# More attention beside each layer block, with the depthwise convolution of that stage on VectorE

## The chip, the cores and the metric

The kernel runs on one core of one Trainium2 chip. A core has five engines with a queue each, which they work off in order: TensorE (PE: matmuls, and the loads of its stationary operand, PEld), VectorE (DVE), ScalarE (ACT), GpSimd (POOL) and SyncE (SP, which here only starts transfers). They meet through semaphores. The metric is the device time in microseconds of one launch, the median of several runs; the profile is of one execution.

## The reference, cut to what matters

Two layers follow each other on `x` of shape 4 x 64 x 64 x 256, in float32.

```python
# layer 0 (DIM 256, INNER 384, 8 states, windows of 2 x 2)
xz = layernorm(x) @ in_proj_W
x_proj, z = xz[..., :384], xz[..., 384:]
windows = window_partition(x_proj, 2)                  # 4 tokens each
y_fwd = light_s6(windows, fwd ...)                     # a scan of 4 steps over 8 states
y_bwd = flip(light_s6(flip(windows), bwd ...))
y_ssm = window_unpartition(0.5 * (y_fwd + y_bwd))
y_dw = depthwise_conv_3x3(x_proj, dw_kernel)           # 384 channels, padding SAME
y_conv = gelu(y_dw @ pw_W)
alpha = sigmoid(gate)
y = (alpha * y_ssm + (1 - alpha) * y_conv) * silu(z) @ out_W
x_out = x + y
x1 = x_out + gelu(layernorm(x_out) @ fuse_W1 + fuse_b1) @ fuse_W2 + fuse_b2

# layer 1: self-attention over the 4096 positions of each image
f, g, hh = x1 @ Wf + bf, x1 @ Wg + bg, x1 @ Wh + bh    # 32, 32, 256 columns
attn = softmax(g @ f.T)                                # 4096 x 4096 for each image
out = gamma * ((attn @ hh) @ Wo + bo) + x1
```

A scan step of `light_s6` is state = dA * state + dBx, y = sum over states of state * c, with dA = exp(dt * a).

## The kernel before

**Tiling.** An image is cut into 8 layer blocks of 8 rows, 512 tokens each (32 blocks for the 4 images). The attention of an image is cut by queries: an early query block is 128 queries against all 4096 keys (32 to an image), a late unit is 256 queries (16 to an image).

**The first layer is one generator.** `first_layer` yields after each small piece of work, and each yield carries a cost in microseconds that the author wrote by hand. For a block `at` it runs `scan(at)`, and beside it, by a credit of SHARE times the scan's costs, `side(at)`: that is the depthwise convolution, the gate and the `tail` of the block before (`conv`, `gate`, `tail(at - 1)`), woven with the head of the block after. `tail` is the pointwise product (L626), the gated combination (L639, L642), the output projection (L649, added at L653), the feed-forward (L669, L680, added at L684), then the keys and queries (L693) and the values (L704, stored after L708). After the scan come `inputs` of the next block (L419, L422) and `merge` (L562, L564).

**The scan.** For each of 8 states and both directions, ScalarE makes the exponentials (L406), TensorE transposes them into a PSUM bank (L462), and VectorE reads the bank into p (L470, L474), carries the state (L492) and adds to y (L485). A bank is free for the next transposes when p was read.

**The depthwise convolution.** For each of three groups of 128 channels it has 9 taps. A tap is either a TensorE matmul of 512 columns with a diagonal matrix (L574), summed in a bank of the ring `q0` to `q3` (`aside`), or a VectorE multiply-and-add over a shifted view of the padded rows (L589 for the first, L595). Before the change image 0 does groups 0 and 1 on TensorE and group 2 on VectorE; images 1 to 3 do six taps of group 0 on TensorE, join them to the other three on VectorE (L591), and do groups 1 and 2 on VectorE.

**Attention beside the layer.** A query block has a preparing generator, `weights`, and a weighted sum, `attend`. `weights` makes the score products in two groups of 16 small matmuls (L844), which take all four banks of the ring at once; ScalarE copies them out (L852), VectorE takes the running maximum (L858, L860, L863, L869), and after two transposes (L867, L871) and a copy (L873) VectorE adds the negative maximum (L877) and ScalarE takes the exponential (L878). `attend` has 8 steps. A step loads two value tiles, does four matmuls into the accumulator (L1036), then moves on its own weights generator and that of the next query block by one piece each, and then lets the first layer run for RATE microseconds of its own costs:

```python
def fill(us):
    debt[0] += us
    while debt[0] > 0:
        cost = next(layer, None)
        ...
        debt[0] -= cost
```

So RATE sets how many query blocks lie beside a layer block. An image's attention begins when the layer has gone through that image; when the whole layer is done, what is left of the queries is done in late units (`late_weights`: L935, L943, L948, L973, L974; `attend_late`: L1014), each of 16 value tiles. `outcome` divides by the sum of the weights and adds the rest (L983, L984).

**What sets the order.** The program writes instructions in the order of these generators; a scheduler that works with priorities then fixes each engine's queue before the launch, and places the semaphore waits. The score products carry a high priority (L839). Value tiles (`vt`) come through SP's queue four ahead, out of five buffers.

Of the kernel before, what the change touches and what calls it, by code (L numbers as in the profile page):

```python
# [34 lines left out]
KI = INNER // P  # L35
# [5 lines left out]
CK = DIM // 8  # L41
EPS = 1e-5
SHARE = 1.2
RATE = 7.2


_VECS = [
# [12 lines left out]
def block_then_attention_kernel(  # L60
# [36 lines left out]
    def v(name, i=0, n=1):  # L97
        a = _AT[name][0] + i
        return vec[:, a : a + n]
# [76 lines left out]
    def aside(shape=(P, TOK)):  # L176

        i = turn[0]
        turn[0] = (i + 1) % 4
        return pss.tile(list(shape), F32, tag=f"q{i}", name=f"q{i}")  # L180
# [383 lines left out]
            nc.vector.scalar_tensor_tensor(xc[:, f, :], py, half_a[:, f : f + 1], xc[:, f, :], ALU.mult, ALU.add)  # L564
            yield 1.1

    def depthwise(ydw, dense, taps):

        for f in range(KI):
            if f < dense:  # L570
                pc = aside()
                for tap in range(taps):
                    dy, dx = divmod(tap, 3)
                    nc.tensor.matmul(  # L574
                        pc, lhsT=diags[9 * f + tap], rhs=xp[:, f, dy : dy + ROWS, dx : dx + W],
                        start=(tap == 0), stop=(tap == taps - 1),
                    )
                    if tap % 3 == 2:
                        yield 2.6
                if taps == 9:  # L580
                    nc.scalar.copy(ydw[:, f, :], pc)
                    continue
            o = ydw[:, f, :].rearrange("p (r c) -> p r c", r=ROWS)
            for tap in range(taps if f < dense else 0, 9):
                dy, dx = divmod(tap, 3)
                x_tap = xp[:, f, dy : dy + ROWS, dx : dx + W]
                w_tap = v("dw", 9 * f + tap)
                if tap == 0:
                    nc.vector.tensor_scalar(o, x_tap, w_tap, None, ALU.mult)  # L589
                elif f < dense and tap == taps:  # L590
                    nc.vector.scalar_tensor_tensor(  # L591
                        o, x_tap, w_tap, pc.rearrange("p (r c) -> p r c", r=ROWS), ALU.mult, ALU.add
                    )
                else:
                    nc.vector.scalar_tensor_tensor(o, x_tap, w_tap, o, ALU.mult, ALU.add)  # L595
                if tap % 3 == 2:
                    yield 2.0
# [3 lines left out]
    def conv(at):  # L601
        b = at // NBLK
        ydw = one.tile([P, KI, TOK], F32, tag="ff", name="ydw")
        ydws[at] = ydw
        yield from depthwise(ydw, KI - 1 if b == 0 else 1, 9 if b == 0 else 6)

    def next_head(at):

# [105 lines left out]
    def side(at):  # L714

        if at == 0:
            yield from late_products()
            yield from next_head(0)
            load_head(2)
            return  # L720
        if at >= NBLK:
            yield from weave(conv(at - 1), 24.0, gate(at - 1, False), 5.2)
        else:
            yield from conv(at - 1)
        yield from weave(tail(at - 1), 46.0, next_head(at), 14.0)
        ready["tail"] = at - 1
# [19 lines left out]
    def first_layer():  # L746
# [22 lines left out]
        for at in range(LAST):  # L769
# [20 lines left out]
            yield from merge(at)  # L790
        yield from drain("tail", LAST - 2)
        yield from conv(LAST - 1)
        yield from gate(LAST - 1, False)
        yield from tail(LAST - 1)
# [27 lines left out]
    def load_values(b, q, n):  # L822

        vt = vp.tile([P, 2, DIM + 1], F32, tag="vt", name="vt")
        a = 2 * (n % 2) * (DIM + 1)
        nc.sync.dma_start(
            out=vt.rearrange("p t c -> p (t c)"), in_=vod[b * NBLK + n // 2][:, a : a + 2 * (DIM + 1)]
        )
        vts[b, q, n] = vt
# [53 lines left out]
# [5 lines that stand above are left out]
            if cost is None:  # L888
                debt[0] = 0.0
                break  # L890
            debt[0] -= cost
# [86 lines left out]
    def outcome(b, q, res, sums):  # L978

        i, t = divmod(q, 4)  # L980
        for c, acc in enumerate(sums):
            rg = st.tile([P, 1], F32, tag="rg", name="rg")
            nc.vector.reciprocal(rg, acc[:, DIM : DIM + 1])  # L983
            nc.vector.scalar_tensor_tensor(res[:, c, :], acc[:, :DIM], rg, res[:, c, :], ALU.mult, ALU.add)  # L984
        a = (t % 2) * DIM
        for wr in range(ROWS // 2):
            nc.sync.dma_start(
                out=ov[b, i, t // 2, wr][:, a : a + len(sums) * DIM],
                in_=res[wr * 32 : (wr + 1) * 32].rearrange("p t c -> p (t c)"),
            )  # L990

    def load_rest(b, q, pool, tag, n):
        i, t = divmod(q, 4)
        res = pool.tile([P, n, DIM], F32, tag=tag, name="res")
        nc.sync.dma_start(
            out=res.rearrange("p t c -> p (t c)"), in_=x1d[b * NBLK + i][:, t * DIM : (t + n) * DIM]
        )
        return res
# [23 lines left out]
    def attend(b, q, es, own, beside, following):  # L1022

        res = load_rest(b, q, two, "res", 1)
        acc = pso.tile([P, TOK], F32, tag="pso", name="acc")
        for k in range(NI):
            for h in range(2):
                n = 2 * k + h
                if n + 4 < 2 * NI:
                    load_values(b, q, n + 4)  # L1030
                else:
                    following(n + 4 - 2 * NI)
                vt = vts.pop((b, q, n))
                for s in range(2):
                    a = (2 * h + s) * P
                    nc.tensor.matmul(  # L1036
                        acc[:, : DIM + 1], lhsT=es[k // 2][:, k % 2, a : a + P], rhs=vt[:, s, :],
                        start=(n == 0 and s == 0), stop=(n == 2 * NI - 1 and s == 1),
                    )
            next(own, None)  # L1040
            next(beside, None)
            fill(RATE)
        outcome(b, q, res, [acc])

# [5 lines left out]
    def twice(pieces):  # L1050

        while True:
            for _ in range(2):
                if next(pieces, 0) == 0:
                    return
            yield
# [7 lines left out]
    own = weights(0, 0, es)  # L1064
    for _ in own:
        fill(RATE)
    a = 0
    while True:
        b, q = divmod(a, NQ)
        b1, q1 = divmod(a + 1, NQ)  # L1070
        if q1 == 0:
            until((b1 + 1) * NBLK - 1)
        ahead = []
        late = ready["tail"] == LAST - 1 and q1 % 2 == 0
        if late:
            n0 = (b1, q1 // 2)
            load_late_queries(*n0)
            beside = twice(late_weights(*n0, 0, ahead))
            attend(b, q, es, own, beside, lambda n: load_late_values(*n0, n))
            es = ahead  # L1080
            break
        if q1 == 0:
            quarter(b1, one, "fQ")
        load_queries(b1, q1)
        beside = weights(b1, q1, ahead)
        attend(b, q, es, own, beside, lambda n: load_values(b1, q1, n))
        es, own = ahead, beside
        a += 1
    odd, block = 0, n0
    while block:  # L1090
        after = ensuing(*block)
        beside, ahead = None, []
        if after:
            load_late_queries(*after)
            beside = late_weights(*after, 1 - odd, ahead)
# [93 lines left out]
```

## Time and profile before

| | |
|---|---|
| median of 3 runs | 5259.01 us (5250.38 to 5259.54) |
| the profiled execution | 5265.47 us |
| its span, first to last instruction | 5263.6 us |
| mean granted TensorE clock | 0.978 |
| PE busy / DVE busy / ACT busy | 4955.8 / 4517.3 / 3571.5 us |
| early query blocks, late units | 74 (296 of L878, 4 each), 27 (216 of L974, 8 each) |
| layer block of image 0, alone | 95 us |
| layer block in the mixed stage, 1128 to 4078 us | 147.5 us, mean of 20 |
| L1036, weighted sum, early | 4736 records, 392 ns mean, 1215.4 us busy |
| L1014, weighted sum, late | 3456 records, 919.7 us busy |
| L574, depthwise taps on TensorE | 576 records, 273.4 us busy |
| L595, depthwise taps on VectorE | 496, 743 ns mean, 357.8 us busy |

How to read it: "busy" is the time in which an engine works on at least one instruction. A float32 matmul of this kernel leaves two records. The mean of one matmul is its own length; since matmuls overlap, a stream of them is closer together than that. An idle engine costs nothing by itself; what matters in a stretch is which engine the others wait for. A group's line gives its busy time, its mean, and, after the last bar, how long the engine idled before it and for whom.

### The profile page before, as it was taken

The numbers are of one execution on the slowest core, as the hardware profiler recorded it, in microseconds if no ns is written. First come the engines' busy times: TensorE is split into PE (matmuls) and PEld (weight loads), VectorE is DVE, ScalarE is ACT, GpSimd is POOL, SyncE is SP. The second block draws the span as 40 slices with busy tenths as digits, with TensorE's granted clock in tenths as the row PEclk, the third lists the DMA queues.
The fourth block names the chain that finished last, engine by engine and source line by source line (L and its number), as shares of the span: only waits on it lengthen the run. The fifth ranks groups of instructions, "written<-read, shape, count | busy, mean of one in ns | idle before, by whom it ended". The sixth has DMA issues, their size and how long they took to land. (4 is left out here: it accounts for less than half of the span.)

```text
span 5263.6 us, 76327 instructions
## 1 busy us (share of the span) xinstructions
PE 4955.8 (94%) x27138; PEld 3543.4 (67%) x27138; DVE 4517.3 (86%) x8256; ACT 3571.5 (68%) x5489; POOL 204.0 (4%) x304
## 2 busy tenths in 40 slices
PE   7999998999999999999999999999999999999999
PEld 4565565666666666666666666666666667888887
DVE  7999999999899988998989988898989866666665
ACT  6778778667777767677777767777777635555554
POOL 0000000000000000000000000000000000000000
PEclk8999999999999999999999999999999999999999
DMA  1010011333333333334333333333333344444444
GB/s 48 26 44 19 23 34 34 102 122 115 118 104 119 113 109 115 114 116 118 118 111 106 119 108 111 118 114 118 112 116 104 112 129 146 147 147 147 147 147 139
DMA packets 330284, 554.14 MB, mean 105 GB/s; under 512 B 51504, under 2 KB 85936, under 8 KB 329904
## 3 DMA queue, kind: packets, MB, share of 16 engines
q1 hardware_dynamic: 326384, 545.40, 34.2%
q8 instruction: 214, 3.51, 0.3%
q10 hardware_dynamic: 3520, 3.87, 0.2%
q14 instruction: 166, 1.36, 0.1%
HBM read 490.28 MB, written 58.79 MB: 104 GB/s over the span
## 5 line engine op out<-in xcount | busy, mean ns | idle before, releaser
L1036 PE MATMUL acc<-vt,eq 128*128 128x257 f32 x4736 | 1215.4, 392 | 17.2 <-issue 7.6
L406 ACT ACTIVATE e<-dt,a_sc 128x384 f32<-128x384 f32 x1536 | 853.3, 611 | 272.8 <-PE bank L462 262.5
L1036 PEld LDWEIGHTS acc<-vt,eq 128*128 128x128 f32 x4736 | 875.0, 195 | 234.2 <-issue 107.6
L462 PEld LDWEIGHTS bank<-ident,e 128*128 128x128 f32 x4320 | 521.2, 143 | 319.5 <-issue 113.4
L462 PE MATMUL bank<-ident,e 128*128 128x128 f32 x4320 | 658.9, 279 | 79.1 <-DVE p L474 37.1
L1014 PE MATMUL bank<-vt,eT 128*128 128x257 f32 x2560 | 645.8, 382 | 0.0
L492 DVE SCALAR_TENSOR_TENSOR h<-u,bc,p 128x384 f32<-128x384 f32 x1024 | 613.4, 613 | 0.4
L485 DVE SCALAR_TENSOR_TENSOR y<-h,bc,y 128x384 f32<-128x384 f32 x960 | 589.0, 614 | 3.2 <-ACT y L483 0.4
L474 DVE TENSOR_TENSOR p<-bank,h 128x384 f32<-128x384 f32 x960 | 517.1, 548 | 55.1 <-PE bank L462 54.5
L1014 PEld LDWEIGHTS bank<-vt,eT 128*128 128x128 f32 x2560 | 478.6, 189 | 83.7 <-issue 13.9
L852 ACT COPY eq<-q 128x512 f32<-128x512 f32 x592 | 308.6, 587 | 192.6 <-PE q L844 117.5
L948 DVE TENSOR_TENSOR mx<-mx,eT 128x512 f32<-128x512 f32 x378 | 261.7, 692 | 152.2 <-ACT eT L943 121.3
L878 ACT ACTIVATE eq<-eq 128x1024 f32<-128x1024 f32 x296 | 308.1, 1053 | 103.0 <-DVE eq L877 100.1
L877 DVE TENSOR_TENSOR eq<-eq,nb 128x1024 f32<-128x1024 f32 x296 | 357.4, 1220 | 7.6 <-ACT nb L873 7.4
L595 DVE SCALAR_TENSOR_TENSOR ydw<-xp,vec,ydw 128x512 f32<-128x512 f32 x496 | 357.8, 743 | 1.4
L943 ACT COPY eT<-q 128x512 f32<-128x512 f32 x432 | 221.5, 597 | 194.7 <-PE q L935 194.7
L860 DVE TENSOR_TENSOR mx<-mx,eq 128x512 f32<-128x512 f32 x444 | 306.5, 690 | 38.4 <-ACT eq L852 31.5
L406 ACT ACT_TABLE_LOAD x241 | 309.2, 1283 | 14.4 <-PE bank L462 10.2
L485 DVE SCALAR_TENSOR_TENSOR y<-p,bc,y 128x384 f32<-128x384 f32 x512 | 313.1, 612 | 0.4
L470 DVE SCALAR_TENSOR_TENSOR p<-bank,bc,u 128x384 f32<-128x384 f32 x480 | 291.6, 608 | 21.1 <-PE bank L462 20.6
L973 DVE TENSOR_TENSOR eT<-eT,m 128x1024 f32<-128x1024 f32 x216 | 247.7, 1219 | 42.3 <-ACT m L970 42.3
L626 PE MATMUL q<-ydw,wpw 128*128 128x512 f32 x576 | 269.5, 602 | 13.3 <-ACT eq L852 12.8
(154 smaller groups left out, 7524.7 us busy)
## 6 DMA issues: line engine op xcount, KB each, us to landing
vt<-vod SPq DMA_DIRECT2D x1616, 257.0 KB, 2.8
vod<-vst SPq DMA_DIRECT2D x32, 514.0 KB, 3.9
xt<-in_x_dram SPq DMA_DIRECT2D x256, 64.0 KB, 1.9
xo<-in_x_dram SPq DMA_DIRECT2D x256, 64.0 KB, 2.3
x1d<-xo SPq DMA_DIRECT2D x32, 512.0 KB, 2.9
res<-x1d SPq DMA_DIRECT2D x74, 128.0 KB, 2.6
out_dram<-res SPq DMA_DIRECT2D x296, 32.0 KB, 1.6
fgd<-fg SPq DMA_DIRECT2D x32, 256.0 KB, 2.1
```

The source lines that it names most:

```text
L406: nc.scalar.activation(e[:, f, :], dts[d][:, f, lo : lo + 3 * P], AF.Exp, scale=a_sc[:, d, f * NST + n : f * NST + n + 1],)
L462: nc.tensor.transpose(pa[:, f * P : (f + 1) * P], es[d, n][:, f, off : off + P], ident)
L474: nc.vector.tensor_tensor(p, pa[:, :INNER], hs[d], ALU.mult)
L485: nc.vector.scalar_tensor_tensor(y[:, t, :], h, c, y[:, t, :], ALU.mult, ALU.add)
L492: nc.vector.scalar_tensor_tensor(hs[d], u[d][:, t, :], bc[:, t, d, n : n + 1], p, ALU.mult, ALU.add)
L595: nc.vector.scalar_tensor_tensor(o, x_tap, w_tap, o, ALU.mult, ALU.add)
L852: nc.scalar.copy(e[:, j, :], pr[2 * a + j])
L860: nc.vector.tensor_tensor(mx, mx, e[:, r % 2, :], ALU.max)
L877: nc.vector.tensor_tensor(e8, e8, nb.unsqueeze(1).broadcast_to([P, 8, P]), ALU.add)
L878: nc.scalar.activation(e, e, AF.Exp)
L1014: nc.tensor.matmul(sums[c][:, : DIM + 1], lhsT=e[:, r % 2, s, c * P : (c + 1) * P], rhs=vt[:, s, :], start=(n == 0 and s == 0), stop=(n == ...
L1036: nc.tensor.matmul(acc[:, : DIM + 1], lhsT=es[k // 2][:, k % 2, a : a + P], rhs=vt[:, s, :], start=(n == 0 and s == 0), stop=(n == 2 * NI ...
```

## The change

Three edits.

1. RATE goes from 7.2 to 5.7: each attention step lets fewer microseconds of the layer pass, so a layer block is spread over more query blocks.
2. `depthwise` takes, for each channel group, how many of its taps go to TensorE. Image 0 keeps (9, 9, 0); images 1 to 3 go from six taps of group 0 to (0, 0, 0): all 27 taps on VectorE.
3. In a step of `attend`, the two generators are moved on before the step's first weighted-sum matmul instead of after its last.

```diff
-RATE = 7.2
+RATE = 5.7
...
-    def depthwise(ydw, dense, taps):
-
-        for f in range(KI):
-            if f < dense:
+    def depthwise(ydw, split):
+
+        for f, taps in enumerate(split):
+            if taps:
                 pc = aside()
                 for tap in range(taps):
                     dy, dx = divmod(tap, 3)
...
-            for tap in range(taps if f < dense else 0, 9):
+            for tap in range(taps, 9):
...
-                elif f < dense and tap == taps:
+                elif tap == taps:
                     nc.vector.scalar_tensor_tensor(
                         o, x_tap, w_tap, pc.rearrange("p (r c) -> p r c", r=ROWS), ALU.mult, ALU.add
                     )
...
-        yield from depthwise(ydw, KI - 1 if b == 0 else 1, 9 if b == 0 else 6)
+        yield from depthwise(ydw, (9, 9, 0) if b == 0 else (0, 0, 0))
...
                 vt = vts.pop((b, q, n))
+                if h == 0:
+                    next(own, None)
+                    next(beside, None)
                 for s in range(2):
                     a = (2 * h + s) * P
                     nc.tensor.matmul(
                         acc[:, : DIM + 1], lhsT=es[k // 2][:, k % 2, a : a + P], rhs=vt[:, s, :],
                         start=(n == 0 and s == 0), stop=(n == 2 * NI - 1 and s == 1),
                     )
-            next(own, None)
-            next(beside, None)
             fill(RATE)
```

## The prediction

> **What bounds the kernel now.** I read the page first (engine totals, the 40 slices), then the chain that ended last, then stretches of the span one by one, then the waits inside the mixed stage. All durations come from one profiled execution: it took 5265.5 us, of which the span is 5263.6 and 1.9 lie around it; the median of the three runs shown is 5259.0, so I add differences to 5259.
>
> ```profile
> PE 4955.8 (94%) x27138; PEld 3543.4 (67%) x27138; DVE 4517.3 (86%) x8256; ACT 3571.5 (68%) x5489; POOL 204.0 (4%) x304
> ...
> PE   7999998999999999999999999999999999999999
> ...
> DVE  7999999999899988998989988898989866666665
> ```
>
> The slices show three stages. Slices 1 to 6 are the first layer alone, image 0; then a mixed stage (the first layer of images 1 to 3 with attention beside it, some 3400 us); from about 4350 us attention alone, where VectorE falls to 6 tenths. The chain gives the price of the last stage: the same two-piece pattern returns every 66.6 us, and it is matmuls only.
>
> ```profile
> 4397.74 2.17 PE bank L1014 x10
> ...
> 4464.34 2.17 PE bank L1014 x10
> ```
>
> That is two late units of 256 queries, so 33.3 us each, or 16.7 us per 128 queries, all TensorE. Now the stretches: 20 layer blocks (1128 to 4078 us, by the second sum of L684) average 147.5 us. One of them, near the mean, cut at the ends of L708, L564, L639, L653, L684 and L708, beside the whole late stage:
>
> ```profile
> 2764.40:2791.10 26.70, 23.44 (x137) 15.70 (x136) 26.30 (x47) 22.93 (x35) 0.00 (x0) 1.00 0.39 119
> 2791.10:2843.10 52.00, 48.63 (x266) 33.28 (x268) 47.21 (x82) 42.06 (x64) 0.00 (x0) 0.93 0.33 99
> 2843.10:2854.00 10.90, 10.90 (x78) 9.38 (x75) 10.84 (x23) 4.20 (x8) 0.00 (x0) 1.00 0.40 125
> 2854.00:2901.70 47.70, 43.37 (x252) 31.12 (x249) 40.07 (x80) 32.81 (x50) 6.88 (x9) 1.00 0.34 102
> 2901.70:2912.40 10.70, 10.53 (x54) 8.31 (x55) 7.28 (x15) 4.80 (x9) 0.00 (x0) 1.00 0.57 188
> ...
> 4366.00:5258.00 892.00, 892.00 (x5193) 729.58 (x5190) 566.23 (x809) 440.75 (x650) 0.00 (x0) 1.00 0.49 146
> ```
>
> (Columns: stretch, length, busy TensorE, its weight loads, VectorE, ScalarE, GpSimd, granted clock, DMA share, GB/s.) What the total hides: a block has two halves. In the first 78.7 us (inputs, merge, the depthwise convolution beside the start of the next scan, gate) VectorE is busy 73.5, and the convolution's VectorE taps lie there and nowhere else. In the last 69.3 us (output projection, feed-forward, values) TensorE is busy 64.8 and VectorE only 58.2. So "TensorE 94%" is true, but VectorE sets the pace of half of every block, and that is the half in which the change gives it more.
>
> ```profile
> DVE p L474 <- PE bank L462: 52.1, 35, 4.4
> ...
> DVE mx L860 <- ACT eq L852: 27.9, 26, 2.1
> ...
> DVE p L470 <- PE bank L462: 19.1, 19, 3.0
> ...
> DVE mx L858 <- ACT eq L852: 17.4, 17, 2.4
> ```
>
> These are waits of those 20 blocks: VectorE loses (52.1 + 19.1 + 27.9 + 17.4) / 20 = 5.8 us per block because TensorE's transposes, or the scores behind them, come late.
>
> **The change part by part.**
>
> *Pace (RATE).* The changed order holds 92 early query blocks where there were 74, and 18 late units where there were 27. No work vanishes; 18 query blocks of 128 move from the late stage into the 24 mixed layer blocks, 0.75 to each. Removed from the end: 9 x 33.3 = 300 us. Price in the mixed stage, by the engine that paces each half. VectorE per query block:
>
> ```profile
> L877 DVE TENSOR_TENSOR eq<-eq,nb 128x1024 f32<-128x1024 f32 x296 | 357.4, 1220 | 7.6 <-ACT nb L873 7.4
> L860 DVE TENSOR_TENSOR mx<-mx,eq 128x512 f32<-128x512 f32 x444 | 306.5, 690 | 38.4 <-ACT eq L852 31.5
> ...
> L595 DVE SCALAR_TENSOR_TENSOR ydw<-xp,vec,ydw 128x512 f32<-128x512 f32 x496 | 357.8, 743 | 1.4
> ```
>
> 4 x 1.22 + 7 x 0.69 (six of L860, one of L858) + 1.5 for L863, L869, L983, L984 = 11.2 us; in the timeline each next instruction starts some 0.08 us before the last one's end (two L485 and L877: 0.61 long, 0.53 apart), 15 instructions, so 10.0. TensorE per query block: 16.7 as in the late stage, plus the smaller shapes' own cost. Scores in 128 columns take 2 x 1.1 us (1.17 for one group in the timeline) against 2.16 for half a late unit, and three 128-column transposes stand for two: 17.0. The first half is 0.53 of a block: 0.40 x 10.0 = 4.0 us. The second: 0.35 x 17.0 = 6.0 us. ScalarE gets 0.75 x 10 us and is 68% busy (42.1 of 52.0 in its fullest stretch): covered; without cover it would be 2 to 3 us per block.
>
> *Depthwise.* In images 1 to 3 six taps of channel group 0 leave TensorE: 144 instructions in all, two records each, 0.43 us apart, 12 x 0.43 = 5.2 us per block. On VectorE the 21 taps (18 of L595, 1 of L591, 2 of L589 at 0.48) become 27 (24 and 3): 5 x 0.743 + 0.48 = 4.2, less 6 x 0.08: 3.7 us per block, all in VectorE's half. The 5.2 us saved on TensorE lie in the same half, where it does not set the pace, so they shorten nothing by themselves. A score bank that held the partial sum, and L591's wait for it (7.0 us in 20 blocks), go too.
>
> *Order in a step.* The own and the next block's pieces now stand ahead of the step's four weighted-sum matmuls. They issue no DMA; the value loads on SP keep their order. Behind the score products now wait the weighted sums, when a score bank is not free: L844 waited 7.7 + 7.4 + 5.0 + 2.7 = 22.8 us in 20 blocks. In the built order the first score group stood on average 2.0 matmuls into a step and now 0.9, because the scores already had high priority. That moves it by 1.1 x 0.475 = 0.5 us. Bounds: twice 0.5 us x 3.9 query blocks = 3.9 us per block gained, if every score came earlier to its waiting maximum, or lost, if every one stood longer on a bank: -94 to +94 us. I take 0: the shift is small beside the bank waits that have both signs.
>
> *DMA.* Value loads rise from 1616 to 1760 of 257 KB. The late stage moves 146 GB/s without one TensorE gap, the mixed stage 112; a fifth more stays below that. Cost 0.
>
> **Sum.** Per block 3.7 + 4.0 + 6.0 = 13.7 us, x 24 = +329; late stage -300: +29. Against it stands relief. In VectorE's half TensorE gets 0.40 x 17.0 - 5.2 = 1.6 us more, while the half grows by 7.7: 6.1 us of new slack for the transposes that VectorE waits for. Of the 5.8 us of such waits per block I take a third away (between 0 and all: 0 to -139 us), because blocks whose first half was already more one-sided lost less in it (by the cost of the instructions between the marks, 6.2 us over VectorE's own in the third of the blocks with the least surplus over TensorE, 3.1 in the third with the most): 2.0 x 24 = -48. Total -19: 5240 us.
>
> A rule that would judge otherwise: the Trainium skill, "Perfetto Trace Analysis", section "Identifying the Most-Contended Engine", says matmul busy time is a poor measure, and to compare VectorE's occupancy with the weight-load share. By it VectorE (86% against 67%) paces the kernel everywhere, and moving a convolution onto it is wrong, though the pace change then pays: 24 x (3.7 + 0.75 x 10.0) - 300 = -31. But the late row has no TensorE gap with weight loads at 730 of 892, 82%: a full TensorE shows that, so neither engine has the mixed stage alone. I keep the two halves.
>
> **The rivals.**
>
> *TensorE paces all of it* (0.14). Then VectorE's work is free, 24 x 5.2 = 125 us go and 18 x 0.3 = 5 come: 5139. For it: 94% busy, idle only 193 us in those 20 blocks. Against: nearly all of that idle time has VectorE busy.
>
> *VectorE's queue holds TensorE back* (0.35). Taps and attention's additions stand in one in-order queue ahead of the scan's p, whose reading frees TensorE's transpose banks. L462 waited for L470 and L474 27.9 + 17.4 us in 20 blocks, 2.3 per block. If the fuller queue doubles that and the relief fails: 5259 + 29 + 55 = 5343, with relief half there 5300. It decides from 1.3 us per block above my sum (31 / 24).
>
> *No change* (0.14): the relief is just 1.2 us instead of 2.0 per block: 5259. That the change does not do what it says is excluded by the built order: 92 and 18.
>
> **How the numbers follow.** My sum has 0.37, own range 5200 to 5248. A measurement of this kernel tells 0.2% (10.5 us) from no change. Faster: 0.37 + 0.14 less a little of the sum's upper edge, 0.50; same 0.15; slower 0.35. The range goes from just above the TensorE rival to the middle of the VectorE one: 5150 to 5320.
>
> **What would show it.** The late stage 18 x 33.3 = 600 us; the mixed block near 159 us (147.5 + 11.7) with VectorE's half near 84.5 and TensorE's near 75; VectorE 96% busy in its half; waits of p for the transposes lower per block. A block of 155 or less would say the relief was larger, one above 161 that VectorE's queue holds TensorE back; then L462 waiting for p would lead TensorE's waits.

## The result, and the profile after

The changed kernel takes 5241.8 us (median of 12 runs, 5239.2 to 5249.4) against 5258.2 for the kernel before (median of 12): a ratio of 0.9974, with a 95% interval from 0.9965 to 0.9983. That is 16.4 us, 0.26% faster, just clear of what a measurement can tell; the forecast was 19 us. The profiled execution has a span of 5245.1 us (5263.6 before).

The page of the changed kernel, engine totals and slices:

```profile
PE 4861.3 (93%) x27444; PEld 3509.2 (67%) x27444; DVE 4585.4 (87%) x8391; ACT 3582.8 (68%) x5508; POOL 208.3 (4%) x304
...
PE   7999998899999999999899999999999889899999
...
DVE  7999999889989989988999988899889898866665
```

TensorE worked 94.5 us less, but the span is only 18.5 us shorter: 76 us of what was saved came back as idle TensorE. VectorE worked 68 us more. The last stage now fills somewhat under five slices instead of seven; its chain keeps the old price:

```profile
4679.02 2.17 PE bank L1014 x10
...
4745.62 2.17 PE bank L1014 x10
```

Again 66.6 us for two late units. Stretches of a block near the mean, cut at the same marks as before (the ends of L708, L564, L639, L653, L684, L708), and of the last stage; the columns are those of the table in the prediction:

```profile
3578.30:3611.00 32.70, 30.09 (x190) 20.05 (x189) 32.33 (x58) 25.56 (x40) 0.00 (x0) 1.00 0.42 124
3611.00:3664.00 53.00, 48.59 (x269) 35.16 (x268) 51.58 (x90) 43.55 (x69) 0.00 (x0) 0.97 0.44 129
3664.00:3676.90 12.90, 11.28 (x83) 9.09 (x82) 12.87 (x28) 6.38 (x11) 0.00 (x0) 1.00 0.32 100
3676.90:3721.80 44.90, 41.60 (x241) 30.18 (x240) 36.74 (x72) 29.55 (x44) 6.41 (x9) 1.00 0.38 114
3721.80:3735.60 13.80, 13.80 (x97) 10.98 (x96) 10.34 (x22) 5.43 (x10) 0.00 (x0) 1.00 0.69 215
...
4655.00:5240.00 585.00, 585.00 (x3399) 479.35 (x3398) 367.42 (x526) 284.60 (x419) 0.00 (x0) 1.00 0.49 146
```

The first two rows are what the prediction called VectorE's half, the next three TensorE's. VectorE is busy 83.9 of the first 85.7 us. Averaged over the 19 blocks in the middle of the mixed stage, cut at the same marks in each trace, the halves are:

| us per block | first half | VectorE busy in it | VectorE idle in it | TensorE busy in it | TensorE at half clock in it | second half | block |
|---|---|---|---|---|---|---|---|
| before | 78.3 | 74.7 | 3.7 | 72.7 | 4.3 | 68.9 | 147.2 |
| changed | 85.5 | 83.3 | 2.2 | 77.5 | 7.8 | 74.5 | 160.0 |
| pace alone | 87.9 | 80.3 | 7.5 | 81.2 | 5.9 | 73.9 | 161.8 |
| taps alone | 80.2 | 78.3 | 1.9 | 69.6 | 8.4 | 67.8 | 148.1 |
| pace and taps | 85.3 | 83.1 | 2.2 | 77.8 | 8.3 | 74.0 | 159.3 |

The column on the clock counts the time in which the trace grants TensorE half its clock. One such stretch lies in the second row of the block above:

```profile
3635.97:3639.38 3.41, 3.41 (x45) 2.71 (x45) 3.41 (x7) 3.37 (x7) 0.00 (x0) 1.00 0.81 246
3639.38:3642.79 3.41, 1.49 (x9) 1.09 (x8) 3.41 (x7) 2.45 (x6) 0.00 (x0) 1.00 0.85 257
3642.79:3646.20 3.41, 3.41 (x10) 2.82 (x10) 3.06 (x6) 2.25 (x3) 0.00 (x0) 0.50 0.08 26
```

TensorE waited 1.92 us for VectorE's p (L462 for L474), was busy for under half of 3.41 us, and had clock 0.50 in the next. The mixed stage of this trace has 50 such stretches, 242 us in all; in the 3.4 us before one TensorE is busy 40% in the mean, in the 3.4 us before that 89%. At half clock the records of L1039 follow each other every 428 ns, otherwise every 217.

Where the time went: from the start to the end of the last block's L708 the span grew from 4323.0 to 4622.8 us (+299.8), and what follows shrank from 940.6 to 622.3 (-318.3).

### The profile page after: what moved, and what is told of

It reads as the page before. It is cut to its first block, busy times and chain, and to the rows that moved or that the text cites. A ratio compares the mean times of both kernels' runs of the same rounds, so it can differ in the third digit from the quotient of the medians.

```text
span 5245.1 us, 77394 instructions
## 1 busy us (share of the span) xinstructions
PE 4861.3 (93%) x27444; PEld 3509.2 (67%) x27444; DVE 4585.4 (87%) x8391; ACT 3582.8 (68%) x5508; POOL 208.3 (4%) x304
## 5 line engine op out<-in xcount | busy, mean ns | idle before, releaser
L1039 PE MATMUL acc<-vt,eq 128*128 128x257 f32 x5888 | 1521.2, 394 | 41.3 <-issue 19.3
L1039 PEld LDWEIGHTS acc<-vt,eq 128*128 128x128 f32 x5888 | 1090.2, 196 | 296.9 <-issue 130.7
L462 PE MATMUL bank<-ident,e 128*128 128x128 f32 x4320 | 662.1, 280 | 105.9 <-DVE p L474 59.1
L462 PEld LDWEIGHTS bank<-ident,e 128*128 128x128 f32 x4320 | 523.4, 143 | 329.4 <-issue 94.3
L852 ACT COPY eq<-q 128x512 f32<-128x512 f32 x736 | 386.1, 588 | 306.7 <-PE q L844 191.4
L474 DVE TENSOR_TENSOR p<-bank,h 128x384 f32<-128x384 f32 x960 | 515.5, 547 | 49.1 <-PE bank L462 48.4
L877 DVE TENSOR_TENSOR eq<-eq,nb 128x1024 f32<-128x1024 f32 x368 | 443.6, 1217 | 23.0 <-ACT nb L873 22.6
L595 DVE SCALAR_TENSOR_TENSOR ydw<-xp,vec,ydw 128x512 f32<-128x512 f32 x640 | 462.8, 742 | 0.4
L1014 PE MATMUL bank<-vt,eT 128*128 128x257 f32 x1728 | 432.3, 382 | 0.0
L860 DVE TENSOR_TENSOR mx<-mx,eq 128x512 f32<-128x512 f32 x552 | 382.5, 693 | 52.7 <-ACT eq L852 45.2
L1014 PEld LDWEIGHTS bank<-vt,eT 128*128 128x128 f32 x1728 | 323.4, 189 | 55.6 <-issue 8.6
L470 DVE SCALAR_TENSOR_TENSOR p<-bank,bc,u 128x384 f32<-128x384 f32 x480 | 291.5, 607 | 17.4 <-PE bank L462 17.0
L844 PE MATMUL q<-gq,fQ 32*128 32x128 f32 x5888 | 246.8, 293 | 35.5 <-ACT eq L852 17.5
L844 PEld LDWEIGHTS q<-gq,fQ 32*128 32x128 f32 x5888 | 202.6, 194 | 105.4 <-ACT eq L852 26.9
L948 DVE TENSOR_TENSOR mx<-mx,eT 128x512 f32<-128x512 f32 x252 | 174.4, 692 | 95.5 <-ACT eT L943 74.8
```

What stands on the lines that cost most here:

```text
L462: nc.tensor.transpose(pa[:, f * P : (f + 1) * P], es[d, n][:, f, off : off + P], ident)
L474: nc.vector.tensor_tensor(p, pa[:, :INNER], hs[d], ALU.mult)
L844: ins = nc.tensor.matmul(pr[r][:, s * P : (s + 1) * P], lhsT=fQ[CK * r : CK * (r + 1), at : at + P], rhs=gq[CK * r : CK * (r + 1), :], sta ...
L852: nc.scalar.copy(e[:, j, :], pr[2 * a + j])
L877: nc.vector.tensor_tensor(e8, e8, nb.unsqueeze(1).broadcast_to([P, 8, P]), ALU.add)
L1014: nc.tensor.matmul(sums[c][:, : DIM + 1], lhsT=e[:, r % 2, s, c * P : (c + 1) * P], rhs=vt[:, s, :], start=(n == 0 and s == 0), stop=(n == ...
```

## The experiments

Each time is given with its distance from the kernel before, measured beside it (5257.3, 5262.4 or 5263.1 us). Where a run changes the changed kernel, its difference to that one is the difference of the two distances from the kernel before; the changed kernel stands at -16.4.

### The three parts, one at a time

Pace alone, on the kernel before:

```diff
-RATE = 7.2
+RATE = 5.7
```

> The kernel before with RATE 5.7 alone (six taps on TensorE, old order). The built order has 94 early query blocks and 17 late units: 20 query blocks move, 0.83 per layer block. Two halves (my theory): 0.44 x 10.0 in VectorE's half and 0.39 x 17.0 in TensorE's is 11.0 us per block, x 24 = +265, and 10 x 33.3 = 333 go from the end: -68. But TensorE gets 7.5 us more in VectorE's half, which grows by 4.4 alone, so its slack shrinks and VectorE's waits for transposes and scores grow by about 2.2 us per block (+53): about 5243. TensorE paces all: 20 x 0.3 = +6: 5264. VectorE's queue holds TensorE back: with the growth of the waits doubled, 5300.

Measured 5300.8: +43.5 us, ratio 1.0080 (1.0065 to 1.0095). The edit that carries the change's gain makes the kernel slower by itself. The stretches of a block near its mean show where:

```profile
1992.70:2023.00 30.30, 28.24 (x157) 18.52 (x156) 29.73 (x53) 22.70 (x34) 0.00 (x0) 1.00 0.39 123
2023.00:2080.50 57.50, 52.07 (x305) 36.77 (x304) 50.25 (x86) 44.43 (x68) 0.26 (x1) 0.97 0.40 119
```

In the second stretch, that of the convolution, TensorE is busy 52.1 us and VectorE 50.3, and the stretch takes 57.5. The reading is that two engines which are nearly full at once and feed each other lose time on both sides; below, TensorE work put into the first half raises VectorE's idle time there too, from 2.2 to 3.8 us. In the changed kernel the same stretch has 48.6 and 51.6 and takes 53.0. VectorE idles 7.5 us per block in this half (table) where it idled 3.7. The expected +2.2 us of waits were +3.9, and more of the moved attention landed in this half than its share of the time (VectorE busy +5.6 us, not +4.4).

Taps alone (all 27 on VectorE in images 1 to 3, RATE 7.2, old order):

```diff
-        yield from depthwise(ydw, KI - 1 if b == 0 else 1, 9 if b == 0 else 6)
+        yield from depthwise(ydw, (9, 9, 0) if b == 0 else (0, 0, 0))
```

> The kernel before with the 27 taps on VectorE in images 1 to 3 alone (RATE 7.2, old order; 74 early query blocks stay). Two halves: +3.7 us per block in VectorE's half, x 24 = +89; TensorE's slack there grows by 8.9 us, which takes about half of the 5.8 us of waits per block, -70: about 5277. TensorE paces all: -125: 5133. VectorE's queue holds TensorE back, without relief: 5347.

Measured 5301.2: +44.0 us, ratio 1.0080 (1.0064 to 1.0097). TensorE loses 5.2 us of work per block and the kernel gets slower: "TensorE paces all" (5133) falls by 168 us. VectorE's work in the first half rose by 3.6 us, just what the sum had (3.7), and its idle time fell by 1.8, to 1.9, which leaves +1.9 us for the half; a relief of 2.9 was expected. The second half is 1.1 us shorter, so these 19 blocks grew by 0.9 us each; of the 36 us between the two profiled spans 28 lie before the end of the last L708, 8 behind it. TensorE's busy time in the first half fell by 3.1 us only, though 5.2 us of work left: it ran 4.1 us more per block at half clock, and half of that makes up the missing 2.1.

Order alone, on the kernel before:

> The kernel before with the new order in a step alone. My theory: 0, 5258 (between 5248 and 5268). If scores that come earlier release VectorE's maxima: down to 5164. If the weighted sums stand longer behind scores that wait for a bank: up to 5352.

Measured 5256.3: -0.9 us, ratio 0.9995 (0.9986 to 1.0003). As expected, nothing.

Pace and taps with the old order, the fourth corner of the square (here against the changed kernel):

```diff
                 vt = vts.pop((b, q, n))
-                if h == 0:
-                    next(own, None)
-                    next(beside, None)
...
+            next(own, None)
+            next(beside, None)
             fill(RATE)
```

> The changed kernel with the old order in a step: pace and taps alone, the fourth corner of that square (92 early query blocks). If the order is worth nothing, as at the old pace (-1 us): 5242. If it is worth what it was beside the new pace and six taps (5301 against 5286): 5256. If pace and taps add up without acting on each other, 5258 + 43 + 44 = 5345; if the taps make room for the pace, as the two halves say, at most 5256.

Measured 5231.2: -31.8 us, ratio 0.9939 (0.9924 to 0.9953). So +43.5 and +44.0 together make -31.8: the two edits act on each other with -119 us. This version is faster than the kernel before by 32 us, and than the changed one by 15.

### Taps at the new pace

Six taps of group 0 back on TensorE, with pace and order:

```diff
-        yield from depthwise(ydw, (9, 9, 0) if b == 0 else (0, 0, 0))
+        yield from depthwise(ydw, (9, 9, 0) if b == 0 else (6, 0, 0))
```

> The changed kernel with six taps of group 0 back on TensorE (pace and order alone; 94 early query blocks, 17 late units). If the order is worth nothing, as in the run of pace alone: about 5243, so that the move of the taps is worth nothing beside the new pace, since what VectorE is spared (3.7 us per block) comes back as waits for a TensorE without slack. TensorE paces all: 5242 + 125 = 5367. VectorE's cost alone, no change of waits: 5242 - 89 = 5153.

Measured 5286.5: +29.2 us, ratio 1.0056 (1.0041 to 1.0071), 46 us slower than the changed kernel. At the old pace the same taps on TensorE gained 44 us. The sign of where a tap is best done turns with the pace.

Three taps instead, `(3, 0, 0)`:

> The changed kernel with three taps of group 0 on TensorE in images 1 to 3 (94 early query blocks, 17 late units). The earlier runs show that in the first half of a block each engine's microsecond costs about a half: TensorE +2.6, VectorE -2.0 is +0.3 us per block, +7, less 3 for the two more query blocks: about 5246. If TensorE alone sets that half at the new pace (six taps there cost 45 us): half of it, 5264. If VectorE alone: 5242 - 24 x 2.0 = 5194.

Measured 5244.3: -18.8 us, ratio 0.9961 (0.9946 to 0.9976). Within 3 us of the changed kernel (with 94 early query blocks here and 92 there): between none and three taps the choice is flat, and the step from three to six costs 48 us.

### What a microsecond costs in each half

Four runs put the same ballast into one half or the other of the changed kernel's blocks, in images 1 to 3. VectorE: four maxima of a 128 x 512 tile with itself, between the taps or on the feed-forward's output. TensorE: six matmuls of 512 columns whose sum the real product overwrites, ahead of the pointwise product or of the feed-forward. The first of each:

```diff
+                if f == 2 and at >= NBLK and tap in (1, 3, 5, 7):
+                    nc.vector.tensor_tensor(ydw[:, f, :], ydw[:, f, :], ydw[:, f, :], ALU.max)
                 if tap % 3 == 2:
                     yield 2.0
...
             pw = aside()
+            for k in range(2 if at >= NBLK else 0):
+                nc.tensor.matmul(
+                    pw, lhsT=wpw[:, k, f * P : (f + 1) * P], rhs=ydw[:, k, :], start=True, stop=True
+                )
             for k in range(KI):
```

VectorE work in the first half:

> The changed kernel with VectorE work added in VectorE's half: in images 1 to 3 four additions per block, each the maximum of a 128 x 512 tile with itself, between the taps of group 2 (the values stay the same). 4 x 0.60 = 2.4 us per block, x 24 = 58. Two halves: +58, 5300. TensorE paces all: 0, 5242. VectorE paces all: 5300.

VectorE work in the second half:

> The same four instructions per block, but in TensorE's half, on the feed-forward's first two channel groups. Two halves: hidden, 0 to +10, 5242 to 5252. TensorE paces all: 0. VectorE paces all: +58, 5300.

TensorE work in the first half:

> The changed kernel with TensorE work added in VectorE's half: in images 1 to 3 six matmuls of 512 columns per block (12 records, 5.2 us) ahead of the pointwise product, whose first matmul overwrites their sum. Two halves: most of it is hidden; TensorE's slack there falls by 5.2 us, which brings back some 0.5 to 1.5 us of VectorE's waits per block: +12 to +36, 5254 to 5278. TensorE paces all: +125, 5367. VectorE paces all: 0.

TensorE work in the second half:

> The same six matmuls per block, but in TensorE's half, ahead of the first feed-forward product. Two halves: +125, 5367. TensorE paces all: +125. VectorE paces all: 0, 5242.

| ballast, per block | measured | against before | against changed | first half | second half |
|---|---|---|---|---|---|
| none (changed) | 5241.8 | -16.4 | | 85.5 | 74.5 |
| VectorE 2.4 us, first half | 5284.7 | +22.2 | +38.6 | 86.7 | 74.3 |
| VectorE 2.4 us, second half | 5233.8 | -28.6 | -12.2 | 85.1 | 74.2 |
| TensorE 5.2 us, first half | 5305.3 | +42.8 | +59.2 | 88.0 | 74.2 |
| TensorE 5.2 us, second half | 5343.9 | +81.4 | +97.8 | 85.4 | 78.7 |

No ballast lengthens a half in which it doesn't stand, and three of the four lengthen their own. In the second half TensorE alone counts: 4.2 of its 5.2 us arrive there, and VectorE's 2.4 us arrive nowhere. In the first half both count: VectorE's 2.4 us cost 1.2 in the 19 middle blocks (38.6 / 24 = 1.6 over all), and TensorE's 5.2 us cost 2.5. The two halves stand, but "VectorE's half" is one that two engines share, at about half a microsecond each. The kernel with idle work in VectorE's second half is 12 us faster than without it, which the two halves do not explain. Its executions had a mean granted clock of 0.976 to 0.978 against 0.972 to 0.974, and its mixed stage 191 us at half clock against 242; what that may be worth is worked out below. Why its clock was higher stays open.

### A pace between, and the idle GpSimd

RATE 6.4 (82 early query blocks):

> The changed kernel with RATE 6.4 (82 early query blocks, 23 late units), between the runs at 7.2 (5301, old order) and 5.7 (5242). If each query block that moves gains the same: 5242 + 10 / 18 x 59 = 5275. If the first ones fill TensorE's slack in the first half and the last ones crowd it, below 5242.

Measured 5269.6: +6.5 us, ratio 1.0013 (1.0006 to 1.0020). Its first half is 80.3 us and its second 73.4. By distances from the kernel before, a straight line from the taps alone (+44) to the changed kernel (-16.4) would have +17 here; it is somewhat below that line and above its end. That is no clean point between, though: the taps alone have the old order, and this run has the lowest granted clock of all, 0.958, with 15.6 us at half clock in the first half of a block. Its second half is 4.5 us longer than that of the kernel before, where the whole move of 18 query blocks brings 5.6, though only 8 were moved. Whether a better pace lies between is not settled.

Four of six products on GpSimd (L419):

```diff
-            nc.vector.tensor_tensor(uT, dts[d][:, f, :], xc[:, f, :], ALU.mult)
+            eng = nc.gpsimd if at >= NBLK and f > 0 else nc.vector
+            eng.tensor_tensor(uT, dts[d][:, f, :], xc[:, f, :], ALU.mult)
```

> The changed kernel with four of a block's six products dt times x (L419, groups 1 and 2, images 1 to 3) on GpSimd, which is idle: 4 x 0.60 = 2.4 us per block taken from VectorE in its half. By the run with VectorE work added there (2.4 us for 39 us in all): -39, 5203. If the slower GpSimd (0.85 us for half such a tile) delays the scan's start by its extra 2 x (1.7 - 0.6) us per direction: +4.4 x 24 = +106, 5309.

Measured 5269.5: +6.4 us, ratio 1.0007 (1.0000 to 1.0014), 23 us slower than the changed kernel, where 39 faster or 106 slower were expected. The groups of that run, by form (busy time, mean ns):

```profile
L420 POOL TENSOR_TENSOR uT<-dt,xc 128x512 f32<-128x512 f32 x96 | 149.8, 1560 | 1375.6 <-ACT dt L389 983.5 <-PE bank L423 247.8 <-DMA out_dram<-res 48.3
...
L596 DVE SCALAR_TENSOR_TENSOR ydw<-xp,vec,ydw 128x512 f32<-128x512 f32 x640 | 495.2, 796 | 0.8
...
L590 DVE TENSOR_SCALAR ydw<-xp,vec 128x512 f32<-128x512 f32 x80 | 45.7, 583 | 0.7 <-PE bank L245 0.7
```

and the same two VectorE groups of the changed kernel:

```profile
L595 DVE SCALAR_TENSOR_TENSOR ydw<-xp,vec,ydw 128x512 f32<-128x512 f32 x640 | 462.8, 742 | 0.4
...
L589 DVE TENSOR_SCALAR ydw<-xp,vec 128x512 f32<-128x512 f32 x80 | 37.2, 478 | 0.7 <-PE bank L245 0.7
```

VectorE gave up 96 products and is busy 22 us longer (4607.6 against 4585.4), because its other instructions became longer while GpSimd worked: the 70 taps of L596 that overlap a product of GpSimd took 1214 ns in the mean, the other 570 took 744. TensorE also waited 17.6 us for GpSimd's products (L423 for L420), and the granted clock was 0.971 against 0.974; how the 23 us divide among the three was not found.

## Why the prediction was right, point by point

*The late stage.* 9 units fewer at 33.3 us: right in price (the chain above). 318 us went from behind the last layer block instead of 300, partly because 1.0 early query blocks lie there and not 1.55 (64 records of L1039 against 99 of L1036).

*The size of the block.* Forecast near 159 us, 84.5 in the first half and 75 in the second: 160.0, 85.5 and 74.5. VectorE is busy 83.3 / 85.5 = 97% in its half, forecast 96%. The first half grew by 7.2, not 5.7: VectorE's work in it rose by 8.6 instead of 7.7, of which the taps are 3.6 and the moved attention 5.0 (forecast 4.0), and 1.4 us of idle time went instead of 2.0. The second grew by 5.6, forecast 6.0.

*The taps' cost on VectorE.* 3.7 forecast; the run of the taps alone has 3.6 us more VectorE work per block in the first half.

*"The 5.2 us saved on TensorE ... shorten nothing by themselves".* Right at the old pace (+44 us, all the same), wrong at the new one. There the six taps on TensorE cost 46 us more than on VectorE, and the ballast of the same 5.2 us cost 59. The sum still came out, since the relief stood in it as a line of its own; but it was booked as a third of the waits of the kernel before, whatever else is done.

*The relief of 2.0 us.* It was 1.4 (VectorE's idle time in the first half went from 3.7 to 2.2 us per block), but its base was wrong. Of the 5.8 us of waits per block that I counted, the larger part lies in the second half, where they cost nothing: in the first half VectorE's idle before L474, L470, L858 and L860 was together some 2 us per block. And the relief belongs to the taps alone: the pace without them raises the idle time to 7.5. Of the prediction's parts, the pace was forecast at 240 - 300 = -60 us and measured at +43.5 alone; the taps at +89 less relief and +44.0; together, with the old order, -31.8. The total was right because those errors are one error, the interaction of -119 us, that I had not cut into parts.

*How much of the hit is luck.* The mechanism held in both halves, but the nearness of 16.4 to 19 is in part chance. Up to the end of the last layer block the span grew by 299.8 us where 329 - 48 = 281 were forecast, and behind it 318.3 went where 300 were: two misses of nearly the same size that cancel. And pace and taps together gained 31.8 us, 13 more than was forecast, while the order took back 15 where 0 was.

*The clock.* No term of the sum had it; TensorE's work was priced at full clock throughout. Where VectorE sets the pace, TensorE pauses, and here a short pause was enough: of the 3.4 us windows at full clock in the changed kernel's mixed stage, cut on the grid of its clock records, all 23 with TensorE busy under 40% were followed by half clock, and of the 969 over 55% five. At the old pace, taking the taps off TensorE raised the time at half clock from 4.3 to 8.4 us per block; beside the new pace it is 7.8, with three taps on TensorE 5.0, with six 5.6, with TensorE ballast in that half 6.1. What this costs no run separates from the rest. Executions of one kernel give a price: the changed kernel took 5239.2 to 5243.1 us in nine executions at a mean clock of 0.973 or 0.974, and 5246.9 to 5249.4 in three at 0.972, some 3 us for each thousandth. That may hold the pause itself as well as the slower clock after it. At that price, which is an estimate, the clock would hold 36 of the 44 us of the taps alone (0.968 against 0.980), 12 of the 43.5 of the pace alone (0.976), 12 against the gain of both (0.974 against 0.978), so some 36 of the 119 us of interaction; and 10 of the 12 us of the ballast in VectorE's second half. It would hold none of the 15 us between the two orders at the new pace and all taps on VectorE: both have 0.974.

*The order.* 0 forecast; -0.9 at the old pace, -14 beside pace and six taps (5300.8 to 5286.5), +15 beside pace and all taps (5231.2 to 5241.8, each against its own run of before). The bounds of 94 us held. The sign changes with the rest. The 15 us lie in the mixed stage (its last L708 ends at 4607.1 us with the old order, at 4622.8 with the new). What is shown is a change of some 15 us either way when the built order of the queues changes; what in the order makes it was not found.

*The waits.* In the mixed stage of the changed kernel (1180.7 to 4220.7 us, 19 blocks), VectorE's waits and TensorE's (in total, times, longest):

```profile
DVE mx L860 <- ACT eq L852: 40.3, 28, 4.5
DVE mx L858 <- ACT eq L852: 40.2, 20, 3.6
DVE p L474 <- PE bank L462: 39.8, 32, 3.3
```

```profile
PE bank L462 <- DVE p L474: 32.3, 30, 3.2
PE bank L462 <- DVE p L470: 31.4, 23, 2.9
```

Waits of p for the transposes fell, as named (L474 from 2.6 to 2.1 us per block), and in VectorE's half, where they count, from 0.8 to 0.2. The maxima's waits for the score copies were not named and rose from 2.3 to 4.2 us per block; most of that lies in the second half, where VectorE has time.

*The rivals.* TensorE pacing everything is refuted by the taps alone and by the two ballast runs in the first half, VectorE pacing everything by the two in the second. No change at all is outside the ratio's interval (0.9965 to 0.9983). VectorE's queue holding TensorE back came in part: TensorE's waits for p rose from 2.3 to 3.4 us per block, not to the 4.6 of that rival, and the block, at 160.0, stayed just below the 161 us named. The other sign named for it does not decide: L462's waits for p lead TensorE's list now, but one of them led it before too (27.9 us for L470 in 20 blocks). The middle figure given for that rival, 5300, doesn't follow from its parts: 5343 less half the relief is 5319. The kernel that did end on the slow side, pace alone with its block of 161.8 us, got there by a full TensorE in VectorE's half, which none of the rivals had.

## What to carry to other kernels

A busy total hides stretches with different limits: cut one repeat of the loop at marks that both engines pass, and price each moved instruction in the stretch that it lands in. Where two engines were both nearly full, a microsecond of either cost about half of itself here; so two edits that fill and empty the same stretch can each lose alone and gain together, and neither is judged without the other. Look at the granted clock of every run before a difference of some 10 us is given a cause. Work can be moved out of a last stage that one engine fills alone, but what it is moved beside sets the price.

## What the runs showed of the hardware that was not expected

VectorE instructions that read two operands from SBUF, and the convolution's first tap, which reads one, became longer while GpSimd multiplied two SBUF tiles: the taps from 742 to 796 ns in the mean, their first tap from 478 to 583. Where they overlap a product of GpSimd they took 1214 and 1393 ns, elsewhere 744 and 480. Those that read one operand from PSUM did not change: L475 took 551 ns in the 18 cases with overlap and 551 in the others. The Trainium skill, "SBUF — State Buffer", section "Who interferes with whom", says that a VectorE instruction with two SBUF inputs contends with GpSimd's reads, since its second input comes through a port that they share, that one with a single SBUF input is spared outside the two-port modes, and that `tensor_scalar`, the first tap's operation, can enter such a mode. The trace agrees with who is slowed and who is spared; the ports themselves it does not show. With 96 products of 1.56 us that took away more than the 96 x 0.60 = 58 us that VectorE was spared.
